# Two graph layers on one core: the first loads in four groups instead of three, with batch 1 ahead of half of the adjacency matrix

## The chip, the cores and the metric

The kernel runs on one core of one Trainium2 chip. The metric is the device time of one execution in microseconds (us), here the median of three runs. Inside the core, TensorE (PE in the profile, with its weight loads as PEld) multiplies matrices, VectorE (DVE) and ScalarE (ACT) work on tiles elementwise, GpSimd (POOL) does small elementwise work, and SyncE (SP) issues the transfers between the chip's memory (HBM) and the on-chip memory. Transfers are run by 16 DMA engines.

## The reference

`x` holds 16 batches of 1024 nodes with 128 features each, `adj` is a dense 1024 x 1024 matrix, and everything is float32. Two layers are applied, each on top of a normalisation and a ReLU:

```
h = relu(layernorm(x))                       # over the 128 features, no scale, eps 1e-5
x = x + adj @ (h @ weight) + bias            # layer 0
h = relu(layernorm(x))
for _ in range(5):                           # layer 1: a gated recurrence
    m  = adj @ h                             # used for "in" and for "out"
    av = concat(m, m)
    u3 = h @ u3_w.T + u3_b
    z  = sigmoid(av @ w3_w.T + w3_b + u3)
    r  = sigmoid(av @ w4_w.T + w4_b + u3)
    hv = tanh(av @ w5_w.T + w5_b + (r * h) @ u5_w.T + u5_b)
    h  = (1 - z) * h + z * hv
x = x + h
```

## The kernel before, in words

**Tiling.** The 16 batches are worked in 8 pairs. A batch is a tile of 128 partitions by 8 chunks of 128 features (1024 nodes). The adjacency matrix is cut into 4 row blocks (`i` from 0 to 3, two chunks each) and two column halves (`g` of 0 and 1). A piece `raw[i][g]` is 128 partitions by 2 chunks by 512 columns, 512 KB. The four pieces with `g = 0` lie in tiles of their own (`raw_0` to `raw_3`), the four with `g = 1` lie in the tail of the large tile `forms`, which is needed for something else only later.

**Stages.** The first two pairs go through layer 0 by plain matmuls (`aggregate_plainly`, the tiles `pq_a`). All later products with the adjacency matrix use a fast scheme for 4 x 4 block matrices: the right-hand operands are sums of adjacency blocks (`right_op`, made once by `adj_sums` on DVE from all eight `raw` pieces), the left-hand operands are sums of blocks of `h` (`forms`), and 26 products take the place of 32. After that come the gates of the recurrence (`pr`, `pv`), five steps for each pair, with two pairs in turn and the next pairs' layer 0 fitted in between.

**The start.** The order of each engine's instructions is fixed by the program: nearly every call goes through `pin`, which keeps program order on its engine. PE first runs six matmul instructions on zeros (`unread`). Then come, for pair 0, batch 0 against the `g = 0` half (8 products, for which the trace has 16 matmul records, two for each float32 product), batch 1 against the same half, then batch 0 and batch 1 against the `g = 1` half, then the same for pair 1 (batches 2 and 3). A product with chunk `c` needs the normalised chunk `hP_a` of the batch and piece `raw[c // 2][g]`.

The normalised chunks come from `normalize(..., in_parts=True)`. DVE computes the statistics of each chunk (`statistics`, `scales`), POOL the power -1/2 (`rstd`), DVE the shift (`nmr`), and ACT the ReLU (`relu`). Batch 0 is done in three parts as its tile lands in three parts, and batch 1 in one go. On DVE the statistics of batch 1 stand ahead of the first three groups of `adj_sums`; the statistics of batches 2 and 3 and the rest of `adj_sums` come behind.

**The transfers.** All are issued from SP in program order. Before the change there are three groups. The first goes out at once: batch 0 in three parts, then the four `g = 0` pieces, of which `raw_0` is in two parts. The other two groups wait for a mark, which is a one-column memset on DVE into the tile that the group's first load then overwrites; that load, and all behind it on SP, have to wait until DVE has come to the memset. `other_loads(0)` holds batch 1 alone, with its mark behind the last statistics of batch 0. `other_loads(1)` holds the four `g = 1` pieces, batches 2 and 3, two pieces that go into `right_op` as they are, the bias `gb`, the weights and the biases, with its mark behind the last `nmr` of batch 0.

The calls that issue the loads and the marks are these. `x_tile` and `load_x` give and fill a batch's tile, `load_adj(i, g)` loads a piece:

Of the kernel before, what the change touches and what calls it, by code (L numbers as in the profile page):

```python
# [8 lines left out]
F32 = mybir.dt.float32  # L9
# [4 lines left out]
P = 128  # L14
# [135 lines left out]
def tile_two_gnn_layers(  # L150
# [9 lines left out]
    nc = tc.nc  # L160
    pin = tc.keep_in_program_order
    B, N, D = x.shape
# [3 lines left out]
    NB = N // BLK  # L166
# [5 lines left out]
    nat = ctx.enter_context(tc.tile_pool(name="nat", bufs=4))  # L172
# [9 lines left out]
    def dma(out, in_):  # L182
        pin(nc.sync.dma_start(out=out, in_=in_))

    def by_slots(ap):
        return ap.rearrange("(p c) d -> p c d", c=NC)

    def x_tile(b):
        return pre.tile([P, NC, D], F32, tag="xt", name=f"xt_{b}")

    def load_x(b, xt=None, parts=((0, NC),)):
        xt = xt or x_tile(b)
        for cs in parts:
            cs = slice(*cs)
            dma(xt[:, cs], by_slots(x[b])[:, cs])
        return xt
# [12 lines left out]

    raw = [[None] * NH for _ in range(NB)]  # L210

    def load_adj(i, g):
        if g == 0:
            t = nat.tile([P, N], F32, tag="hN", name=f"raw_{i}")
        else:
            first = len(FORM) - (NB - i) * 2 * SB
            t = forms[:, first : first + 2 * SB].rearrange("p s j d -> p (s j d)")
        raw[i][g] = t.rearrange("p (c n) -> p c n", c=SB)
        parts = SB if (i, g) == (0, 0) else 1
        for k in range(parts):  # L220
            cs = bass.ts(k, SB // parts)
            dma(raw[i][g][:, cs], adjT[:, bass.ts(i, SB), bass.ts(g, HALF)][:, cs])
# [2 lines left out]
    w_sb = const.tile([P, 9, D], F32, tag="w", name="w_sb")  # L225
    b_sb = const.tile([P, 5], F32, tag="b", name="b_sb")
    xts = {0: load_x(0, parts=((0, 2), (2, CH), (CH, NC))), 1: x_tile(1)}
    for i in range(NB):
        load_adj(i, 0)


# [1 line left out]
    def other_loads(k):  # L233
        if k == 0:
            pin(nc.vector.memset(xts[1][:, 0, 0:1], 0.0))
            load_x(1, xts[1])
            return
        first = len(FORM) - NB * 2 * SB
        pin(nc.vector.memset(forms[:, first, 0, 0:1], 0.0))
        for i in range(NB):  # L240
            load_adj(i, 1)
        for b in range(2, 4):
            xts[b] = load_x(b)
        for name, i, j in SINGLES:
            dma(right_op[:, RIGHT[name]], adjT[:, bass.ts(i, SB), bass.ts(j, BLK)])
        dma(gb, gbias.to_broadcast([P, D]))
        dma(w_sb, weights)
        dma(b_sb, biases)
# [48 lines left out]
    def normalize(dst, src, nm, then, in_parts=False):  # L297

        stats, mv, ve, rstd, nmr = {}, {}, {}, {}, {}
        every, first, second = range(NC), range(CH), range(CH, NC)

        def statistics(i, cs):
            if i not in stats:
                stats[i] = small.tile([P, NC, 6], F32, tag="stats", name=f"stats_{nm}{i}")
            for c in cs:
                pin(nc.vector.bn_stats(stats[i][:, c, :], src[i][:, c, :]))  # L308

        def scales(i, cs=every):  # L310
            if i not in mv:
                mv[i] = small.tile([P, NC, 2], F32, tag="mv", name=f"mv_{nm}{i}")
                ve[i] = small.tile([P, NC], F32, tag="ve", name=f"ve_{nm}{i}")
                rstd[i] = small.tile([P, NC], F32, tag="rstd", name=f"rstd_{nm}{i}")
                nmr[i] = small.tile([P, NC], F32, tag="nmr", name=f"nmr_{nm}{i}")
            for c in cs:
                pin(nc.vector.bn_aggr(mv[i][:, c, :], stats[i][:, c, :]))
            part = slice(cs[0], cs[-1] + 1)
            pin(nc.vector.tensor_scalar_add(ve[i][:, part], mv[i][:, part, 1], EPS))
            pin(nc.gpsimd.tensor_tensor(rstd[i][:, part], ve[i][:, part], mhalf[:, part], ALU.pow))  # L320

        def shift(i, cs=every):
            part = slice(cs[0], cs[-1] + 1)
            pin(
                nc.vector.scalar_tensor_tensor(
                    nmr[i][:, part], mv[i][:, part, 0], -1.0, rstd[i][:, part], ALU.mult, ALU.mult
                )
            )

        def relu(i, cs=every):  # L330
            for c in cs:
                pin(
                    nc.scalar.activation(
                        dst[i][:, :, c, :],
                        src[i][:, c, :].rearrange("p (a e) -> p a e", e=SQ),
                        AF.Relu,
                        bias=nmr[i][:, c : c + 1],
                        scale=rstd[i][:, c : c + 1],
                    )
                )  # L340

        yield ANY
        if in_parts:
            a, b = range(2), range(2, CH)
            for cs in (a, b):
                statistics(0, cs)
                scales(0, cs)
            shift(0, a)
            relu(0, a)
            statistics(0, second)  # L350
            scales(0, second)
            other_loads(0)
            shift(0, b)
            relu(0, b)
            shift(0, second)
            relu(0, second)
            other_loads(1)
            statistics(1, every)
            scales(1)
            shift(1)  # L360
            relu(1)
            return
        statistics(0, first)
        yield ANY
        statistics(0, second)
        yield ANY
        scales(0)
        yield ANY
        statistics(1, first)
        yield ANY  # L370
        shift(0)
        statistics(1, second)
        for i in range(2):
            for k in range(CH):
                yield ANY
                relu(i, range(2 * k, 2 * k + 2))
                if (i, k) == (0, 0):
                    scales(1)
                elif (i, k) == (0, 2):
                    shift(1)  # L380
            then(i)
# [248 lines left out]
    def prelude(pair, kept=None):  # L630
# [20 lines left out]
        if kept is not None:  # L651
            bias_of[pair] = lambda: [add_bias(i) for i in range(2)]
        then = add_bias if kept is None else lambda i: None
        yield from normalize(h0, xt, f"a{pair}", then, in_parts=pair == 0)
        background["h"] = h0
        yield BLOCK
# [24 lines left out]
        def park(i):  # L681
# [4 lines left out]
            parked[pair].append((scratch, blocks))  # L686

        yield from normalize(hN, xt, f"b{pair}", park)
        if kept is not None:
            kept[pair] = hN  # L690
# [290 lines left out]
```

## Time and profile before

| | |
|---|---|
| median of 3 runs | 1825.98 us (1825.83 to 1826.25) |
| the profiled execution, its own time | 1827.61 us |
| its span, from the first to the last instruction | 1825.80 us |
| PE busy | 1815.9 us, 99% of the span |
| DVE busy | 1388.9 us, 76% |
| ACT busy | 759.3 us, 42% |
| POOL busy | 124.9 us, 7% |
| loads and stores | 145.15 MB, 79 GB/s over the span |
| mean granted PE clock | 0.998 |

The profile is of one execution, whose time is 1.81 us longer than its span. Busy shares are averages over the whole span; the change touches the first microseconds alone, so the views that count are those of that stretch: the instructions in order of time, the waits, and busy time and granted clock in narrow windows. Times in these views are microseconds from the start of the span. A row of the view in order of time names engine, line, operation and tiles, merges neighbours of one kind (`x12`), and ends with the idle time of the engine before it and what ended that.

### The profile page before, as it was taken

Reading aid. Unit: us, or ns where it says so; the run is one execution under the profiler, and the core shown is the slowest. Engines: PE = TensorE matmul, PEld = TensorE weight load, DVE = VectorE, ACT = ScalarE, POOL = GpSimd, SP = SyncE. Lnnn points to the kernel's source line nnn. Section 1 sums busy time; section 2 is a strip of 40 time slices with the busy share of each in tenths; the row PEclk is TensorE's granted clock in tenths of the full one; section 3 lists DMA queues with packets and bytes.
Section 4 is the critical chain, followed back from the end, with each engine's and each line's share of the span. In section 5 each row is a group of like instructions: output and inputs, shape, how many; then the busy total and the mean of one; then the engine's idle time right before and its main releaser. Section 6 shows DMA issues by size and latency. Waiting matters only on the chain.

```text
span 1825.8 us, 20644 instructions
## 1 busy us (share of the span) xinstructions
PE 1815.9 (99%) x6810; PEld 1272.9 (70%) x6810; DVE 1388.9 (76%) x3265; ACT 759.3 (42%) x1487; POOL 124.9 (7%) x169
## 2 busy tenths in 40 slices
PE   8999999999999999999999999999999999999999
PEld 3676777677776687668766668666866677776666
DVE  6787777777878787778778878787868777766677
ACT  3354354435334434443434533453344333333433
POOL 4202001100002000200000200020000000000000
PEclk9999999999999999999999999999999999999999
DMA  4241113111632113111362111311153312111123
GB/s 164 70 138 47 46 62 100 46 47 52 198 120 69 47 47 114 49 46 47 101 187 93 58 54 39 116 47 46 47 161 105 104 58 70 58 46 47 47 69 116
DMA packets 87803, 145.15 MB, mean 79 GB/s; under 512 B 9744, under 2 KB 65168, under 8 KB 87696
## 3 DMA queue, kind: packets, MB, share of 16 engines
q1 hardware_dynamic: 87696, 143.83, 24.8%
q8 instruction: 54, 0.88, 0.2%
q14 instruction: 53, 0.43, 0.1%
HBM read 77.73 MB, written 66.06 MB: 79 GB/s over the span
## 4 chain that ended last, share of the span: by engine, by line
PE 97%; DVE 2%; DMA 0%; POOL 0%; issue 0%; ACT 0%; DVEq 0%
PE pr L705 23%; PE bT L426 22%; PE pv L705 15%; PE bV L426 11%; PE bX L426 7%; PE bD L426 4%; PE bT_a L426 3%; PE pq_a L545 3%; PE bF L426 2%; PE bJ L426 2%; PE bV_a L426 2%; PE po L666 2%; PE bX_a L426 1%; PE bD_a L426 1%; DMA xt<-in_x_dram 0%; DVE stats_a L308 0%
## 5 line engine op out<-in xcount | busy, mean ns | idle before, releaser
L426 PE MATMUL bT<-right_op,forms 128*128 128x256 f32 x1920 | 454.9, 379 | 0.0
L426 PEld LDWEIGHTS bT<-right_op,forms 128*128 128x128 f32 x1920 | 363.9, 190 | 64.5 <-issue 8.4
L705 PE MATMUL pr<-mT,w_sb 128*128 128x512 f32 x640 | 307.3, 592 | 0.5 <-DVE mT L453 0.5
L426 PE MATMUL bV<-right_op,forms 128*128 128x256 f32 x960 | 228.0, 379 | 0.0
L705 PEld LDWEIGHTS pr<-mT,w_sb 128*128 128x128 f32 x640 | 121.5, 190 | 136.9 <-issue 132.5
L717 ACT ACTIVATE r<-pr,bsum 128x512 f32<-128x512 f32 x160 | 109.7, 686 | 246.6 <-PE pr L705 246.3
L718 DVE TENSOR_TENSOR r<-r,hT 128x512 f32<-128x512 f32 x160 | 110.7, 692 | 127.2 <-ACT r L717 125.5
L426 PEld LDWEIGHTS bV<-right_op,forms 128*128 128x128 f32 x960 | 181.3, 190 | 24.1
L740 ACT ACTIVATE hv<-pv,bsum 128x512 f32<-128x512 f32 (+1 forms) x161 | 110.3, 685 | 163.7 <-PE pv L705 163.7
L705 PE MATMUL pv<-mT,w_sb 128*128 128x512 f32 (+1 forms) x322 | 163.6, 589 | 0.0
L705 PE MATMUL pv<-r,w_sb 128*128 128x512 f32 (+1 forms) x322 | 163.6, 589 | 0.0
L705 PE MATMUL pr<-hT,w_sb 128*128 128x512 f32 x320 | 163.4, 592 | 0.0
L744 DVE TENSOR_TENSOR hv<-hv,hT 128x512 f32<-128x512 f32 x156 | 105.8, 678 | 73.4 <-ACT hv L740 73.4
L426 PE MATMUL bX<-right_op,forms 128*128 128x256 f32 x640 | 157.7, 379 | 0.0
L426 PEld LDWEIGHTS bX<-right_op,forms 128*128 128x128 f32 x640 | 121.1, 190 | 16.2
L746 DVE TENSOR_TENSOR hT<-hT,hv 128x512 f32<-128x512 f32 (+1 forms) x161 | 110.9, 689 | 16.7 <-PE pv L705 0.5
L725 ACT ACTIVATE z<-pr,bsum 128x512 f32<-128x512 f32 x160 | 110.1, 688 | 20.2 <-PE pr L705 20.2
L705 PEld LDWEIGHTS pv<-r,w_sb 128*128 128x128 f32 x322 | 61.2, 190 | 76.2 <-issue 59.8
L705 PEld LDWEIGHTS pr<-hT,w_sb 128*128 128x128 f32 x320 | 60.8, 190 | 76.5 <-issue 76.5
L705 PEld LDWEIGHTS pv<-mT,w_sb 128*128 128x128 f32 x322 | 61.0, 190 | 76.1 <-issue 75.6
L745 DVE TENSOR_TENSOR hv<-hv,z 128x512 f32<-128x512 f32 x156 | 107.9, 692 | 5.4
L582 DVE STREAM_TRANSPOSE sq<-hT 128x512 f32<-128x512 f32 x156 | 101.2, 687 | 0.0
(175 smaller groups left out, 2279.0 us busy)
## 6 DMA issues: line engine op xcount, KB each, us to landing
fn<-sq SPq DMA_DIRECT2D x78, 512.0 KB, 2.9
hN<-fn SPq DMA_DIRECT2D x312, 128.0 KB, 3.5
ft<-hP_b SPq DMA_DIRECT2D x64, 128.0 KB, 2.4
x1d<-xt SPq DMA_DIRECT2D x16, 512.0 KB, 3.2
sqt<-ft SPq DMA_DIRECT2D x16, 512.0 KB, 5.5
x<-x1d SPq DMA_DIRECT2D x16, 512.0 KB, 5.3
xt<-in_x_dram SPq DMA_DIRECT2D x15, 512.0 KB, 6.6
out_dram<-x SPq DMA_DIRECT2D x14, 512.0 KB, 2.7
```

What stands on the lines that cost most here:

```text
L426: nc.tensor.matmul(halves(bank)[:, half], forms[:, FORM[form], c, :], right_op[:, RIGHT[name], c, :], start=bool(opens) and c == 0, stop=c ...
L545: nc.tensor.matmul(bank, hN[i][:, c, :], raw[c // SB][g][:, c % SB], start=c == 0, stop=c == NC - 1,)
L582: pin(nc.vector.transpose(squares_of_half(sq, g), transposed_half(hT, g)))
L666: nc.tensor.matmul(pt[:, j, :], aT[i][:, bass.ts(g * CH + j, P)], w_sb[:, WG, :], start=True, stop=True,)
L705: nc.tensor.matmul(bank, w_sb[:, w, :], moving, start=start, stop=stop, skip_group_check=True)
L717: pin(nc.scalar.activation(r, pg, AF.Sigmoid, bias=bsum[:, 1:2]))
L718: pin(nc.vector.tensor_mul(r, r, view(hT, u)))
L725: pin(nc.scalar.activation(z[u], banks[u], AF.Sigmoid, bias=bsum[:, 0:1]))
L740: pin(nc.scalar.activation(hv, pg, AF.Tanh, bias=bsum[:, 2:3]))
L744: pin(nc.vector.tensor_sub(hv, hv, h))
L745: pin(nc.vector.tensor_mul(hv, hv, z[u][:, part]))
L746: pin(nc.vector.tensor_add(h, h, hv))
```

## The change

There are now four groups:

- at once: batch 0 in three parts, `raw_0` in two parts, `raw_1`;
- `other_loads(0)`: batch 1, then `raw_2`. Its mark on DVE, in the tile of batch 1, moves up to stand behind the statistics of batch 0's first part (two chunks);
- `other_loads(1)`, new: `raw_3`. Its mark, in the tile of `raw_3`, stands where the mark of batch 1 stood, behind the last statistics of batch 0;
- `other_loads(2)`: what was the last group, with the same content and order. Its mark in `forms` stands now between the statistics of the first four and of the last four chunks of batch 1, so DVE comes to it only once batch 1 has landed.

So in the order of the SP queue, batch 1 moves from behind `raw_3` to between `raw_1` and `raw_2`, and nothing else changes places there. On DVE one memset comes in, one changes its tile and one moves. The orders on PE, ACT and POOL are the same as before, instruction for instruction.

```diff
-    def load_adj(i, g):
-        if g == 0:
+    def load_adj(i, g, t=None):
+        if g == 0 and t is None:
             t = nat.tile([P, N], F32, tag="hN", name=f"raw_{i}")
-        else:
+        elif g == 1:
             first = len(FORM) - (NB - i) * 2 * SB
...
     xts = {0: load_x(0, parts=((0, 2), (2, CH), (CH, NC))), 1: x_tile(1)}
-    for i in range(NB):
+    for i in range(2):
         load_adj(i, 0)
...
     def other_loads(k):
         if k == 0:
             pin(nc.vector.memset(xts[1][:, 0, 0:1], 0.0))
             load_x(1, xts[1])
+            load_adj(2, 0)
+            return
+        if k == 1:
+            raw_3 = nat.tile([P, N], F32, tag="hN", name="raw_3")
+            pin(nc.vector.memset(raw_3[:, 0:1], 0.0))
+            load_adj(3, 0, raw_3)
             return
         first = len(FORM) - NB * 2 * SB
         pin(nc.vector.memset(forms[:, first, 0, 0:1], 0.0))
...
             for cs in (a, b):
                 statistics(0, cs)
                 scales(0, cs)
+                if cs is a:
+                    other_loads(0)
             shift(0, a)
             relu(0, a)
             statistics(0, second)
             scales(0, second)
-            other_loads(0)
+            other_loads(1)
             shift(0, b)
             relu(0, b)
             shift(0, second)
             relu(0, second)
-            other_loads(1)
-            statistics(1, every)
+            statistics(1, first)
+            other_loads(2)
+            statistics(1, second)
             scales(1)
```

## The prediction

> **What bounds the kernel now.** I read the chain of work that ended last first, then PE's waits, then the start in order of time. The chain's first line, by engine:
>
> ```profile
> PE 97%; DVE 2%; DMA 0%; POOL 0%; issue 0%; ACT 0%; DVEq 0%
> ```
>
> PE sets the end, so a microsecond taken out of PE's start is taken off the end, unless PE later meets another engine that didn't move with it. PE's waits over the whole span (who waited for whom: total us, times, longest):
>
> ```profile
> PE pq_a L545 <- ACT hP_a L333: 3.3, 1, 3.3
> PE unread L203 <- DVE zeros L200: 1.5, 1, 1.5
> PE pq_a L545 <- DMA raw<-in_adjT_dram: 0.8, 1, 0.8
> PE pr L705 <- DVE mT L453: 0.5, 1, 0.5
> PE pf L856 <- DVE hT L746: 0.3, 1, 0.3
> ```
>
> The largest by far is the first: PE has finished batch 0 with the first half of the matrix and waits for batch 1's first normalised chunk. In order of time, PE alone:
>
> ```profile
> 5.88 2.42 PE L545 MATMUL pq_a<-raw,hP_a 128*128 128x512 f32 x4
> 9.05 5.39 PE L545 MATMUL pq_a<-raw,hP_a 128*128 128x512 f32 x12 [0.76 <-DMA raw<-in_adjT_dram]
> 17.77 10.17 PE L545 MATMUL pq_a<-raw,hP_a 128*128 128x512 f32 x16 [3.33 <-ACT hP_a L333]
> 27.78 13.90 PE L545 MATMUL pq_a<-forms,hP_a 128*128 128x512 f32 x32
> ```
>
> The reader is to see two losses. The wait of 3.33 us; and the 16 records behind it, which take 10.01 us until the next row starts, where 32 equal ones take 13.90, 0.43 each. At that pace 16 need 6.88, so 3.13 us are lost after the wait. The windows say why (columns: window and length, then busy us of PE, PEld, DVE, ACT, POOL, granted PE clock, DMA share, GB/s):
>
> ```profile
> 6.85:10.27 3.42, 2.66 (x7) 0.99 (x6) 0.17 (x2) 1.96 (x5) 0.42 (x1) 1.00 1.00 358
> 10.27:13.68 3.41, 3.41 (x9) 1.52 (x8) 0.79 (x5) 0.00 (x0) 0.00 (x0) 1.00 1.04 406
> 13.68:17.09 3.41, 0.76 (x2) 0.00 (x0) 1.63 (x15) 0.00 (x0) 1.64 (x1) 1.00 1.06 401
> 17.09:20.50 3.41, 2.73 (x4) 1.18 (x5) 3.41 (x7) 3.27 (x9) 0.00 (x0) 0.50 1.03 400
> 20.50:23.91 3.41, 3.41 (x5) 1.35 (x4) 3.34 (x6) 0.39 (x1) 0.00 (x0) 0.50 0.67 231
> ```
>
> After a window in which PE was busy 0.76 of 3.41 us the clock is 0.50 for two windows. And what the wait hangs on:
>
> ```profile
> 12.89 1.64 DVE L308 BATCH_NORM_STATS2 stats_a<-xt 128x6 f32<-128x128 f32 x8 [5.41 <-DMA xt<-in_x_dram]
> 15.36 1.64 POOL L320 TENSOR_TENSOR rstd_a<-ve_a,mhalf 128x8 f32<-128x8 f32 x1 [8.09 <-DVE ve_a L319]
> 17.02 0.17 DVE L325 SCALAR_TENSOR_TENSOR nmr_a<-mv_a,rstd_a 128x8 f32<-128x8 f32 x1 [1.75 <-POOL rstd_a L320]
> ```
>
> DVE idled 5.41 us for batch 1's tile. From there to PE's restart at 17.77 is a fixed chain of 4.88 us.
>
> **What the Trainium skill says.** "TensorE: Matmul & The Clock Gate", Part 1: The HAM clock gate, says the PE clock halves after about one idle window of 3.4 us, returns after one busy window, and that windows run freely, unrelated to the kernel's start. The trace agrees: 3.41 us windows, 0.50 for 6.83 us. "DMA: Bandwidth & Descriptors", Queues, rings and completion order, says each DMA engine takes a queue's descriptors in ring order. The trace agrees: on SP's one queue landings follow issue. Issues at 3.07, 3.54, 4.05 and 6.24 with times to landing of 5.9, 6.7, 7.5 and 6.6 us put `raw_1` at 9.0, `raw_2` at 10.2, `raw_3` at 11.5, batch 1 at 12.8; the `forms` pieces follow at 14.1, 15.5, 16.8 and 18.1. One 512 KB load takes a slot of about 1.3 us.
>
> **The change part by part.**
>
> *Transfers.* Sizes are equal, so the slots stay and their owners change: `raw_1` 9.0, batch 1 10.2, `raw_2` 11.5, `raw_3` 12.8. This needs issue in time. Mark 1 follows DVE's first `ve` (done 3.93); with the 0.11 us from mark to issue that the old mark showed (6.13 to 6.24), batch 1 is issued at about 4.05 and `raw_2` at 4.4, while the engines work on `raw_0` and `raw_1` until 9.0. Mark 2 stands where the old mark was, so `raw_3` goes at 6.25. No bubble.
>
> *Batch 1.* Statistics start at 10.3 instead of 12.89. The chain is 4.88 us plus one 0.06 us memset in its middle: hP_a is ready for PE at 15.24.
>
> *Batch 0.* `raw_2` comes 1.3 us later than before. From 9.05, four records (chunks of `raw_1`) last until 10.77; PE then waits for 11.5 plus the 0.1 us that the first wait showed, so until about 11.65 (0.9 us, new). Eight records follow, 3.44 us, to 15.09; `raw_3`, needed at 13.37, landed at 12.8. Cost on the path: nothing, because batch 1 isn't ready before 15.24. If that cover were gone it would be 0.9.
>
> *PE's restart.* Idle 0.15 us (15.09 to 15.24) instead of 3.33. Busy shares of the windows until then are about 74% and more, like the 78% after which the clock stayed at 1.00, so I take full clock: 16 x 0.43 = 6.88, and the `g = 1` products start at 22.12 instead of 27.78. Sum: 17.77 - 15.24 = 2.53 for the wait, 3.13 for the clock, **5.66 us**.
>
> *Mark 3.* It is queued behind four statistics of batch 1: 10.3 + 0.87, so about 11.2; SP issues the first `forms` piece at 11.3 instead of 7.52, and everything behind it on SP waits with it (the other three, batches 2 and 3, two right-hand pieces, gb, weights, biases). The slot begins at 12.8. The shortest time from issue to landing in this stretch, 2.3 us for 128 KB, bounds the start-up from above: a bubble of 0 to 0.8 us. I take 0.2, and the last `forms` piece lands at 18.3, batches 2 and 3 at 19.6 and 20.9. PE needs the first piece at 22.1: hidden. SP's waits for earlier landings (3.9 us on `forms` before) don't bind, since those have landed.
>
> *DVE behind it.* It reaches `adj_sums` at 14.6 instead of 17.11, but the first sum needs the second `forms` piece (15.7), the third needs the third (17.0), and the fifth the fourth, so it starts at 18.4 instead of 19.52. From there DVE is 1.1 us early while PE is 5.66 early. So PE gains 4.6 us on DVE, and that is where the stall could go. Next needs: batch 2's chunks (PE 41.51, then 35.85): `nmr` 30.87 becomes 29.8, ACT's eight at 0.4 us finish at 33.2, slack 2.6. Batch 3's ReLUs on ACT end at 36.9 instead of 41.6, which delays one `mT` copy by 0.85 us to 37.5, needed at 40.2. The bias adds on POOL (32, 16.91 us from 34.34) start at 33.2 and end at 50.1; batch 0's are done at 37.5 for its DVE add at 40.45, batch 1's at 41.7 for 41.3. POOL's `rstd_b` then waits for it (51.85 becomes 50.1, not 46.2), and batch 1's `nmr_b` is ready at 55.4, needed by ACT at 57.0. DVE's next `forms` sums start at 60.9 against 60.2, for the product that uses them at 70.4. All slacks positive: cost nothing, but some are only 0.3 to 3 us wide, and the adds of batch 1 slip 0.4 us behind a 0.8 us margin on the PSUM bank.
>
> *Memsets.* One more, 0.06 us on DVE at 3.9. It delays batch 0's first chunks by as much, ahead of the wait for `raw_1` at 9.05: hidden.
>
> **Sum.** Span 1825.80 - 5.66 = 1820.14; the profiled execution 1827.61 becomes 1821.95. The median of the runs lies 1.63 below that execution; the same difference from 1825.98 gives 1820.3. I say **1820.4**. A difference under 0.2% (3.65 us, below 1822.33 or above 1829.63 to count) can't be told from no change.
>
> **The rivals.**
>
> *A, the forecast*, 72%: 1820.4, own range 1819.4 to 1822.0. A quicker slot for `raw_2` and batch 1 gains up to 0.6 more; half a slow window less in the timed runs than in the profile costs 1.6.
>
> *B, the wait goes and the clock gain doesn't*, 14%: the slow stretch isn't in the timed runs of before (their 1.63 us distance from the profiled execution is about one slow window's loss), or the new wait at 10.8 brings it back. Against: three runs within 0.42 us, while freely running windows should scatter them. Gain 2.53: 1823.4.
>
> *C, DVE and POOL hold PE back*, 5%: PE gains only what POOL gains, 1.75: 1824.2. Against: the slacks above.
>
> *D, the order of landing doesn't change*, 4%: loads share the engines and batch 1 still lands near 12.8. Then PE restarts at 17.8: 1826.0.
>
> *E, slower*, 5%: the last group comes too late. DVE can't do the statistics of batches 2 and 3 before its sums have the fourth `forms` piece. Beyond 20.9 (18.3 + 2.6) each further microsecond stalls PE ahead of batch 2, and beyond 26.6 it eats all 5.66: slower from there, by over 0.2% from 30.2. The queue would have to stand 8 us; the 0.8 above speaks against.
>
> **How the numbers follow.** The time is A's. The range, 1819.4 to 1823.4, holds A and B. Faster by over 0.2%: A, and the part of B where half the clock loss goes (1821.9), 0.76. Within: the rest of B, C, D and half of E, 0.20. Slower: 0.04.
>
> **What would show it.** Batch 1's statistics start near 10.3; PE waits for `raw` twice, the second time about 0.9 us near 10.8; its wait for hP_a shrinks to below 0.5; granted clock 1.00 from 6.85 on; the `g = 1` products start near 22.1; `forms` issues near 11.3; DVE's fifth sum near 18.4. Wrong if the clock drops again, if batch 1 lands after 11, or if PE shows a new wait between 35 and 60.

## The result, and the profile after

| | before | after |
|---|---|---|
| median of 12 runs | 1826.36 us (1825.32 to 1827.34) | 1822.01 us (1821.55 to 1822.56) |
| ratio, with its 95% interval | | 0.9976 (0.9967 to 0.9985) |
| the profiled execution, its own time | 1827.61 us | 1821.55 us |
| its span | 1825.80 us | 1819.8 us |

The change makes the kernel 4.35 us faster by the medians, 0.24%. The two profiled executions lie 6.06 us apart. The 1.7 us between these two differences has two parts: the profiled execution before lay 1.25 us above its median, and the profiled execution after was the fastest of the 12 runs, 0.46 us below their median. A second profile of the kernel after, used below, was at the other end (1822.61, the slowest of 14).

The first line of the chain of the kernel after, and PE's waits over its whole span:

```profile
PE 98%; DVE 2%; DMA 0%; issue 0%; ACT 0%; DVEq 0%
```

```profile
PE pq_a L554 <- DMA raw<-in_adjT_dram: 1.5, 3, 0.7
PE unread L203 <- DVE zeros L200: 1.4, 1, 1.4
PE pr L714 <- DVE mT L462: 0.3, 1, 0.3
PE pf L865 <- DVE hT L755: 0.3, 1, 0.3
```

The wait for `hP_a` that led the list is gone. What is left at the start are three short waits for pieces of the matrix. In order of time, PE in the kernel after:

```profile
6.39 1.96 PE L554 MATMUL pq_a<-raw,hP_a 128*128 128x512 f32 x4 [0.51 <-DMA raw<-in_adjT_dram]
8.65 1.96 PE L554 MATMUL pq_a<-raw,hP_a 128*128 128x512 f32 x4 [0.30 <-DMA raw<-in_adjT_dram]
11.27 10.61 PE L554 MATMUL pq_a<-raw,hP_a 128*128 128x512 f32 x24 [0.66 <-DMA raw<-in_adjT_dram]
21.71 13.90 PE L554 MATMUL pq_a<-forms,hP_a 128*128 128x512 f32 x32
```

The third row holds the rest of batch 0 (8 records) and all of batch 1 (16) without a gap between them, and 24 records in 10.44 us until the next row are 0.43 each, the full pace. The `g = 1` products start at 21.71 instead of 27.78, and 6.07 us is, to 0.1, what the span lost. The granted clock of the kernel after, in windows laid on this execution's own clock step (columns as before):

```profile
5.55:8.96 3.41, 2.60 (x7) 0.97 (x6) 1.55 (x12) 1.81 (x5) 1.01 (x1) 1.00 1.00 347
8.96:12.38 3.42, 2.76 (x7) 1.05 (x6) 2.38 (x18) 0.94 (x3) 0.06 (x1) 1.00 1.01 338
...
1818.03:1819.77 1.74, 0.00 (x0) 0.00 (x0) 0.00 (x0) 0.00 (x0) 0.00 (x0) 0.50 0.14 49
```

The clock falls only at the very end, from 1818.03 on, when PE has nothing left to do. Counted back from there in steps of 3.41 us, the windows at the start are those shown: PE is busy 2.60 and 2.76 of 3.41 us in them, and the clock stays at 1.00. The DVE rows of the kernel after, with two of the three marks, batch 1's statistics and the first sum:

```profile
3.83 0.06 DVE L235 MEMSET xt<- 128x1 f32 x1
...
9.83 1.08 DVE L314 BATCH_NORM_STATS2 stats_a<-xt 128x6 f32<-128x128 f32 x5 [1.60 <-DMA xt<-in_x_dram]
10.65 0.06 DVE L245 MEMSET forms<- 128x1 f32 x1
...
16.43 0.69 DVE L281 TENSOR_TENSOR right_op<-forms 128x512 f32<-128x512 f32 x1 [2.27 <-DMA forms<-in_adjT_dram]
```

Batch 1's statistics start 3.06 us earlier, the last group is issued at 10.75, and DVE then waits 2.27 us for it, which it didn't before.

### The profile page after: what moved, and what is told of

It reads as the page before. It is cut to its first block, busy times and chain, and to the rows that moved or that the text cites. A ratio compares the mean times of both kernels' runs of the same rounds, so it can differ in the third digit from the quotient of the medians.

```text
span 1819.8 us, 20644 instructions
## 1 busy us (share of the span) xinstructions
PE 1812.6 (100%) x6810; PEld 1273.2 (70%) x6810; DVE 1391.5 (76%) x3266; ACT 759.0 (42%) x1487; POOL 124.8 (7%) x169
## 4 chain that ended last, share of the span: by engine, by line
PE 98%; DVE 2%; DMA 0%; issue 0%; ACT 0%; DVEq 0%
PE pr L714 23%; PE bT L435 22%; PE pv L714 15%; PE bV L435 11%; PE bX L435 7%; PE bD L435 4%; PE bT_a L435 3%; PE pq_a L554 3%; PE bJ L435 2%; PE bF L435 2%; PE bV_a L435 2%; PE po L675 2%; PE bX_a L435 1%; PE bD_a L435 1%; DMA raw<-in_adjT_dram 0%; PE bJ_a L435 0%
```

## The experiments

Each kernel was measured beside the kernel before, in three sets; within a set all kernels ran on one chip. The medians of the kernel before were 1826.22 (first set, 40 runs), 1826.02 (second, 52) and 1825.97 (third, 24).

### How much is the clock: matmuls on zeros in the wait

```diff
+    def filler():
+        for n in (HALF, HALF, HALF, BLK):
+            pin(nc.tensor.matmul(unread[:, 0:n], zeros[:, 0:P], zeros[:, 0:n], start=True, stop=True))
+
+    put(2, filler)        # kernel before; on PE between batch 0 and batch 1
```

> The kernel before, with four more matmuls on zeros on PE between batch 0 and batch 1 (8 records, some 3.1 us at 0.43 for the long ones), while PE would wait for batch 1. The wait stays, only the clock is kept up. The forecast's sum (3.13 us of clock loss in every run): 3.1 us faster than before, about 1823.2, and full clock from 6.85 on. The theory that the windows fall differently from run to run, so that the runs of before lose only about 1.4 us on average (4.35 measured less 2.94 for the wait): about 1824.9. No part played by the clock: 1826.4.

Measured: 1824.63 us (1824.05 to 1825.40), ratio 0.9992 (0.9984 to 1.0001), an interval that just takes in 1. PE in this kernel:

```profile
14.63 3.17 PE L893 MATMUL unread<-zeros 128*128 128x512 f32 x8
18.12 7.13 PE L545 MATMUL pq_a<-raw,hP_a 128*128 128x512 f32 x16 [0.33 <-ACT hP_a L333]
25.10 13.90 PE L545 MATMUL pq_a<-forms,hP_a 128*128 128x512 f32 x32
```

The filler's four matmuls show as 8 records. (The `unread` matmuls at the kernel's start are, likewise, three and not six; six is the number of their records.) Batch 1 is as late as ever, but its 16 records now take 6.98 us instead of 10.01. So against the profile of before the gain is 3.03 us, as forecast, and yet the median moves by 1.59 only: close to the second theory's 1.4, not to the forecast's 3.1. The runs of the kernel before in this set say why. Sorted by the mean granted clock that each run lists:

| mean granted clock | runs of before | median | range |
|---|---|---|---|
| 1.000 | 9 | 1824.31 us | 1823.93 to 1824.97 |
| 0.999 | 26 | 1826.30 us | 1825.69 to 1826.63 |
| 0.998 | 5 | 1827.85 us | 1827.46 to 1827.88 |

One window of 3.41 us at half clock lowers the mean over 1825 us by 0.0009, so by this reckoning these are runs with no, one and two such windows. The profiled execution of the kernel before, with its 0.998, was one of the rarest kind. In the second set the same three groups held 10, 34 and 8 of 52 runs. With the filler all 13 runs list 1.000, and they lie in or just above the range of the first row; their slowest, 1825.40, is faster than each of the 31 runs in the other two rows. The sorting has one blur: half clock at the very end, as in the profile of after, lowers the mean too without costing PE anything. That is probably why 6 of the 113 runs of the kernels below with a new order of loads list 0.999 too, though they lie among the others of their kernel.

### The mark alone

```diff
-            other_loads(1)
-            statistics(1, every)
+            statistics(1, first)
+            other_loads(1)
+            statistics(1, second)     # kernel before; order of loads as it was
```

> The kernel before, with only the last group's mark moved behind the first four statistics of batch 1; the order of loads stays. The forecast: nothing on PE, 1826.4, as batch 1 still lands in its slot near 12.8; the fourth forms piece lands 1.5 to 2 us later than 18.1, hidden. The rival, that batch 1 shares the engines with the last group in the kernel before: batch 1 lands 0.5 us or more earlier and the time falls by as much or, if the clock stays up, by 2 us or more.

Measured: 1826.39 us, ratio 1.0000 (0.9992 to 1.0008): nothing. Rows of DVE and PE, then windows laid on this execution's own clock steps:

```profile
13.41 1.09 DVE L308 BATCH_NORM_STATS2 stats_a<-xt 128x6 f32<-128x128 f32 x5 [5.96 <-DMA xt<-in_x_dram]
```

```profile
18.32 8.83 PE L546 MATMUL pq_a<-raw,hP_a 128*128 128x512 f32 x16 [3.34 <-ACT hP_a L333]
26.99 13.90 PE L546 MATMUL pq_a<-forms,hP_a 128*128 128x512 f32 x32
```

```profile
15.08:18.49 3.41, 0.17 (x1) 0.17 (x2) 0.88 (x10) 0.71 (x2) 1.64 (x1) 1.00 0.83 270
18.49:21.90 3.41, 3.41 (x5) 1.35 (x6) 2.02 (x4) 2.94 (x8) 0.00 (x0) 0.50 1.06 402
21.90:25.31 3.41, 3.41 (x10) 1.50 (x9) 3.35 (x6) 0.00 (x0) 0.00 (x0) 1.00 1.03 394
```

Although nothing of the last group was issued before 14.34, batch 1 landed no earlier than before. So the last group's loads aren't what made it late. That it was late because two pieces stood ahead of it is what the next kernels test. The windows show the kind of execution that the profile of before missed: the same wait of 3.34 us, but one slow window and not two. The 16 records take 8.67 us, 1.79 over the full pace.

### The order alone, and no marks

The first kernel puts the last group's mark back ahead of batch 1's statistics:

```diff
-            statistics(1, first)
             other_loads(2)
-            statistics(1, second)
+            statistics(1, every)      # kernel after
```

> The changed kernel with the mark of the last group back where it was before (ahead of batch 1's statistics), so only the order of the loads is changed. The forecast: the order does it all; batch 1's statistics start near 9.8, PE as in the changed kernel, 1822.0; the forms pieces land about 1.3 us earlier (fourth near 17.7 instead of 19.0). The rival, that the last group's mark protects batch 1 from loads that share the engines: batch 1 lands 1 to 2 us later, 1823.5 to 1826.

The second issues all loads at once in the order of the kernel after and has no memset at all.

> The changed kernel's order of loads, all issued at once with no mark at all. The forecast: 1822.0, as the order in the queue alone sets when a load lands; the first sum on DVE is no longer late. The rival, that loads in flight share the engines: batch 1 lands later than 11, PE waits 1 to 3 us, 1823.5 to 1825.

Measured: 1821.81 us, ratio 0.9978 (0.9969 to 0.9987), and 1822.40 us, ratio 0.9980 (0.9972 to 0.9988). Both intervals overlap that of the change. So the order in the queue brings nearly all of the gain, and the last group's wait for batch 1 none of it. The other two marks may bring a little: in this one set the kernel without any mark is 0.59 us slower than the first, and all of its 14 runs are slower than 7 of that kernel's 11. Why is open. Batch 1's statistics started at 10.71 and 10.51 in these two profiles, within what single executions of the same order show (9.83 and 10.93 in the two profiles of the kernel after). The price of the last mark: DVE's first sum waits 1.31 us for its load in both, and 2.27 with the mark. Counted from the start of batch 1's statistics that sum comes 1 us sooner without the mark, not the 1.3 forecast.

### One place later in the queue

```diff
-            load_x(1, xts[1])
             load_adj(2, 0)
+            load_x(1, xts[1])         # kernel after: raw_1, raw_2, batch 1, raw_3
```

> The changed kernel with batch 1 one place later in the queue, behind raw_2 (raw_1, raw_2, batch 1, raw_3). The forecast's slots: batch 1 lands about 1.3 us later than in the changed kernel, at 11.1, so its first chunk is ready at 16.0; batch 0 ends at 14.3 as raw_2 comes earlier; PE idles 1.7 us with the clock kept, the g = 1 products start 1.2 us later: 1823.2. The rival, that a single load's place doesn't matter once it is out of the last group's way: 1822.0.

Measured: 1823.19 us, ratio 0.9984 (0.9977 to 0.9990). PE:

```profile
9.61 5.77 PE L554 MATMUL pq_a<-raw,hP_a 128*128 128x512 f32 x12 [1.42 <-DMA raw<-in_adjT_dram]
17.00 7.13 PE L554 MATMUL pq_a<-raw,hP_a 128*128 128x512 f32 x16 [1.61 <-ACT hP_a L339]
23.97 13.90 PE L554 MATMUL pq_a<-forms,hP_a 128*128 128x512 f32 x32
```

A slot is worth what the sum of slots said, 1.2 us, by the medians (1823.19 less 1822.01). The profiled execution was the slowest of the 21 (1824.28), so its times are to be set beside the slow profile of the kernel after, where the `g = 1` products start at 22.82: 1.15 us. A wait of 1.61 doesn't bring a slow window: all 21 runs list a clock of 1.000.

### What a late last group costs

```diff
-            statistics(1, first)
-            other_loads(2)
-            statistics(1, second)
+            statistics(1, every)
             scales(1)
             shift(1)
+            other_loads(2)            # kernel after
```

> The changed kernel with the last group's mark moved further back on DVE, behind batch 1's shift (near 14.0 instead of 10.65), so the last group and with it the DVE sums come some 3.3 us later. The forecast's slack (2.6 us until batch 2's chunks, and a margin of 0.8 us on the PSUM bank counted apart): PE loses at most 0.7, about 1822.7. The theory from the profile after, that the bank of the first layer-0 product has no margin left (its add on DVE comes at once behind the sums, and PE's four products already take 3.90 instead of 3.73): every microsecond counts, PE waits about 3 us in line po, about 1825.

Measured: 1825.26 us (1824.47 to 1826.45), ratio 0.9995 (0.9987 to 1.0004): 3.25 us above the kernel after. The mark came at 14.71 here against 10.65, but batch 1 itself landed later in this execution (10.45 against 9.83); counted from batch 1's statistics the mark is 3.44 us later. The waits of PE that are new, then the rows of ACT and of DVE that stand behind them:

```profile
PE po L674 <- DVE xt L683: 1.5, 1, 1.5
...
PE po L674 <- ACT mT_a L564: 1.4, 1, 1.4
```

```profile
38.24 3.19 ACT L339 ACTIVATE hP_a<-xt,nmr_a,rstd_a 128x128 f32<-128x128 f32 x8 [0.59 <-DVE nmr_a L331]
41.34 0.57 ACT L564 COPY mT_a<-pq_a 128x512 f32<-128x512 f32 x1
```

```profile
43.90 0.94 DVE L281 TENSOR_TENSOR right_op<-raw,right_op 128x512 f32<-128x512 f32 x1
44.76 0.68 DVE L683 TENSOR_TENSOR xt<-po,xt 128x512 f32<-128x512 f32 x1
```

There are two waits and not one. PE's second product `po` waits for a copy on ACT that stands behind batch 3's ReLUs, which wait for DVE. Its fourth waits for the bank of the first (a bank is the part of PSUM, PE's output memory, that one product fills), which DVE empties only behind its eight sums. Of batch 2's chunks, where the forecast put the loss, PE has no wait.

To take the second of the two away, the sums were moved behind the adds:

```diff
-    put(7, later(two, 5), lambda: adj_sums(15, 19))
-    put(8, lambda: adj_sums(19, 23), lambda: bias_of[1]())
+    put(7, later(two, 5))
+    put(8, lambda: bias_of[1]())
...
-    put(2, later(one, 2))
-    put(3, later(one, 2))
+    put(2, later(one, 2), lambda: adj_sums(15, 19))
+    put(3, later(one, 2), lambda: adj_sums(19, 23))
```

> The same late mark, with the eight sums that stand on DVE ahead of those adds (the groups 15 to 18 and 19 to 22) moved behind them. If the PSUM bank behind the sums is the cause of the loss: back to 1822.0 to 1822.7. If another lateness is (batch 2's chunks, POOL's bias adds): still about 1825.

Measured: 1823.48 us, ratio 0.9986 (0.9980 to 0.9993), between the two expectations. PE:

```profile
38.77 1.05 PE L674 MATMUL po<-w_sb,mT_a 128*128 128x128 f32 x8
41.31 2.94 PE L674 MATMUL po<-w_sb,mT_a 128*128 128x128 f32 x24 [1.49 <-ACT mT_a L564]
```

The wait for the bank is gone, and with it 1.78 us of the 3.25. The wait for ACT's copy stayed, 1.49 us. My theory had named one of two causes.

### A version built on this

Order as in the slot experiment, batch 1 normalised in two halves so that its first chunk needs half the statistics, the last group's mark moved ahead of batch 0's last shift, and the eight sums behind the adds as above.

```diff
             relu(0, b)
+            other_loads(2)            # order of loads and sums as above
             shift(0, second)
             relu(0, second)
-            statistics(1, first)
-            other_loads(2)
-            statistics(1, second)
-            scales(1)
-            shift(1)
-            relu(1)
+            statistics(1, first)
+            scales(1, first)
+            statistics(1, second)
+            scales(1, second)
+            shift(1, first)
+            relu(1, first)
+            shift(1, second)
+            relu(1, second)
```

> A version meant to beat both: the order of the last one, with batch 1 normalised in two halves (first chunk ready some 1.5 us sooner after landing), the last group's mark ahead of that, and the eight sums moved behind the adds. Forecast: PE's g = 1 products start 0.4 us before those of the changed kernel and the four products of line po take 3.73 again: 1821.4. The rival, that batch 0 stays what ends last and nothing is gained: 1822.0.

Measured: 1821.31 us (1821.09 to 1821.72), ratio 0.9973 (0.9962 to 0.9983). PE:

```profile
12.82 8.99 PE L557 MATMUL pq_a<-raw,hP_a 128*128 128x512 f32 x20 [0.20 <-DVE ve_a L325]
21.65 13.90 PE L557 MATMUL pq_a<-forms,hP_a 128*128 128x512 f32 x32
...
38.82 3.73 PE L678 MATMUL po<-w_sb,mT_a 128*128 128x128 f32 x32
```

The four products `po` take 3.73 us again. That stands against a kernel after that was measured in another set, so both were measured once more side by side:

> The changed kernel itself once more, beside the next one on the same chip and in the same call. Expected: 1822.0 again, no slow window, and a gain over before that depends on how many slow windows the runs of before had (about 6 against two, 4.3 against one, 2.3 against none).

> The version of e8_best once more, beside the changed kernel. Expected if its gain is real: 0.5 to 0.7 us below the changed kernel, about 1821.3; if the difference of the earlier calls was chance, within 0.2 us of it.

Measured: the kernel after 1821.87 us (1821.45 to 1822.61), ratio 0.9978 (0.9970 to 0.9986); the version 1821.53 us (1820.98 to 1821.92), ratio 0.9976 (0.9967 to 0.9985). In the two comparisons it is 0.70 and 0.34 us faster than the change. The intervals of the ratios overlap almost wholly; that it is faster at all is likely, and 0.3 to 0.7 us is all that these runs can say. Which of its four edits brings that wasn't tested.

## Why the prediction was right, and where it was off

The direction, the path and the span came out as the forecast's sum had them; the median is 1.6 us above the one given. It lies at the upper edge (1822.0) of the range that the forecast, A, gave itself, and well inside the stated range because that was made wide enough to hold rival B. By the forecast's own steps, in the two profiles of the kernel after, which were of its fastest and of its slowest execution:

| step | forecast | profile after | second profile |
|---|---|---|---|
| batch 1's statistics start | 10.3 | 9.83 | 10.93 |
| PE's new wait for `raw_2` | 0.9 | 0.66 | 0.62 |
| PE between batch 0 and batch 1 | 0.15 idle | none | none |
| clock, from 6.85 to the end of the start | 1.00 | 1.00 | 1.00 |
| `g = 1` products start | 22.1 | 21.71 | 22.82 |
| DVE's fifth sum | 18.4 | 19.01 | 20.25 |
| DVE's add of the second `po` | 41.7 | 44.19 | 45.43 |
| span | 1820.14 | 1819.8 | 1820.8 |
| median | 1820.4 | 1822.01 | 1821.87 |

That the span of the first of them meets the forecast within 0.4 us is in part luck: the middle of the two is 1820.3.

*Transfers.* Right: slots keep their times and change their owners. Batch 1 landed at 9.8 (issued at 3.93, 5.9 to landing), `raw_2` at 11.1, `raw_3` at 12.4. The order alone gave nearly the whole gain, one place later cost the 1.2 us forecast, and the last group's mark alone gave nothing.

*PE's restart, the clock term.* This is the term that was mis-sized. "16 x 0.43 = 6.88 ... 3.13 for the clock" is true of the profiled execution and not of the runs. By the sorting above only 5 of 40 runs of before have two slow windows; most have one, 9 have none. By the filler's median the clock is worth 1.59 us, about half of the term. That leaves 2.62 us (1824.63 less 1822.01) for the wait, where the forecast had 2.53. Likewise, the nine runs of before without a slow window lie 2.3 us above the median after. The prediction gave this as rival B, argued from the 1.63 us between the profiled execution and the median, and then gave it 14% because three runs agreed within 0.42 us, "while freely running windows should scatter them". By their times those three were all of the commonest kind: 40 runs span 3.95 us. With 26 of 40 in that group, three in a row from it are nothing rare, about one case in four (an estimate, 0.65 to the third power). A's own range has the term too, as "half a slow window less", for 1.6 us; by half of 3.41 us that is one whole window. The wrong step is the last of the sum, where the 1.63 us was carried over to the kernel after as if it were a constant offset of profiling. The kernel after has no such distance (profiled 1821.55, median 1822.01), because it has no slow windows (all 12 runs list 1.000). The Trainium skill, "TensorE: Matmul & The Clock Gate", Part 1: The HAM clock gate, says that the windows run freely; so a wait of 3.3 us would meet windows of 3.41 us differently from run to run, and the groups above agree. The prediction had drawn this and trusted three runs against it. It also says that the clock returns after one busy window and that the trace agrees; in that trace the window at half clock that was busy 2.73 of 3.41 us was followed by another one at half clock. A sum of 2.53 plus one window (half of 3.41, 1.7) gives 4.2, against 4.35 measured (an estimate, made afterwards).

*Mark 3.* Its bubble was bounded by 0.8 us and taken as 0.2. The first `forms` piece was issued at 10.75 and took 4.2 us, landing at 15.0, 1.3 us behind its slot (12.4 plus 1.3). The 2.3 us that served as the bound belonged to a quarter-size load. With its own 1.3 us of transfer taken off, this one needed 2.9 us to get going, against 1.6 us between its issue and the end of the load ahead. Hidden, as forecast: PE needs the piece at 21.7.

*DVE behind it.* That PE's lead over DVE would cost nothing was nearly true, and by less than the text made of it. The four products `po` took 3.90 us for 3.73, so 0.17 was lost. The forecast's margins were in the wrong place: it made rival E hang on batch 2's chunks, with 2.6 us of slack. The late mark shows the loss at two others, the copy on ACT and the bank of the first product, and there 3.44 us of delay cost 3.25, so next to no slack was left. It had both in its list of needs, "needed at 40.2" and "a 0.8 us margin on the PSUM bank", and treated them as side issues. Rival E's point of decision was therefore too late by more than 2 us. With the late mark nearly all of the gain goes (0.9995); slower than before, as E had it, no kernel here was.

*The bias adds on POOL.* They were spread evenly, 16.91 us over 32, which put the second add on DVE at 41.7. POOL's busy windows in the kernel after, while DVE runs its sums, and then behind them:

```profile
33.83:40.90 7.07, 7.07 (x9) 1.00 0.01 2
40.90:46.00 5.10, 5.10 (x13) 1.00 0.00 0
```

At most nine adds in the first 7.07 us, 0.79 or more each, and about 0.4 each after. The mean hid two paces, and batch 1's adds ended some 2.4 us later than worked out. PE had already passed that place. In the kernel with the sums moved behind the adds the same 32 adds took 13.24 us instead of 16.93.

*Memsets.* Hidden, as forecast.

Rivals C and D found no support: PE's later waits in the kernel after are short ones that were there before (0.3 us), and the order of landing did change.

## What to carry to other kernels

In a queue that is served in order, moving a load is a trade of slots: write down the landing times, swap the owners, and ask of each consumer what it waits for last. A wait near the length of the clock's window can cost a different amount from run to run (here none, one or two slow windows), so one profiled execution can't price it; sort the runs by their mean granted clock before a sum is carried from a profile to a median. When the engine that sets the end is moved forward, list every place where it meets another engine later and take the smallest margin, including copies that stand behind other work and banks that wait to be emptied.

## What the runs showed of the hardware

- The clock's penalty came in whole windows. Runs of the kernel before fell into groups with medians of 1824.3 to 1824.6, 1825.9 to 1826.3 and 1827.3 to 1827.9 us in the three sets, with mean clocks of 1.000, 0.999 and 0.998. In windows laid on each execution's own clock steps, PE windows busy 0.76 and 0.17 of 3.41 us were followed by half clock; those busy 2.66 (before), 2.60 and 2.76 (after) and 1.90 (batch 1 one place later, from 13.49) were not. Going back up took a fuller window: at half clock, one busy 2.73 was followed by half clock again, and two busy all of their 3.41 (before, and the mark alone) by full clock. These are single cases.
- A load that finds the queue empty pays for it: 4.1 us from issue to landing for 512 KB when nothing was ahead of it (the mark alone), against a slot of 1.3 in a full queue.
- DVE and POOL slowed each other. DVE's sums took 0.94 us beside POOL's adds and 0.68 without them. The Trainium skill, "SBUF — State Buffer", Who interferes with whom, says that a DVE instruction with both of its inputs in the on-chip memory contends with a POOL instruction that reads that memory, and the rows agree: with the sums moved behind the adds, the same sums but the first took 0.67 to 0.69 and the adds 0.45 instead of about 0.8. In the kernel after, one small DVE instruction even took 2.58 us where the same instruction took 0.17 in the kernel before, there behind POOL's run of adds. It ended within 0.1 us of the end of that run (33.83 plus 16.93):

```profile
48.20 2.58 DVE L325 TENSOR_SCALAR ve_b<-mv_b 128x8 f32<-128x8 f32 x1
```

  That it was held up through several of POOL's instructions is argued from these times. The first sum of the kernel with the sums moved fits: it started beside the adds, took 3.76 us, and ended 0.55 us behind their last. No run was made to test it.
